# A state-space layer's scan on one core: its convolution summed in PSUM, its decays multiplied into C, and its slots in a new order

## The chip, the cores and the metric

The kernel runs on one core of a Trainium2 chip. The metric is the device time of one execution in microseconds (us). A core has five engines, each with its own queue of instructions that it works off in order: PE (TensorE, matrix products; its weight loads are listed as PEld), DVE (VectorE), ACT (ScalarE), POOL (GpSimd) and SP (SyncE, which here issues DMA transfers). They work on two memories, SBUF and PSUM. PE writes to PSUM, and PSUM has 8 banks of 512 fp32 columns by 128 partitions. An engine waits for another by semaphores.

## The reference

Four layers follow each other on x of shape (4, 128, 64, 64). Only the second is touched. It takes a map of 128 channels through a 1x1 layer, a depthwise 3x3 convolution and silu, then runs two state-space scans (mamba2), forward and backward, over the 4096 pixels of each image:

```python
def _mamba2(u, W_in, conv_w, conv_b, dt_bias, A_log, D, norm_w, W_out):
    zxbcdt = u @ W_in
    z = zxbcdt[..., :DI]
    xBC = zxbcdt[..., DI:DI + DI + 2 * DS]
    dt = zxbcdt[..., -NH:]
    xBC = jax.nn.silu(_causal_dwconv1d(xBC, conv_w, conv_b))
    xs = xBC[..., :DI]
    Bm = xBC[..., DI:DI + DS]
    Cm = xBC[..., DI + DS:]
    dt = jax.nn.softplus(dt + dt_bias)
    dA = jnp.exp(dt * -jnp.exp(A_log))
    xh = xs.reshape(b, l, NH, HD)
    dtx = dt[..., None] * xh
    def step(h, inp):
        dA_t, dtx_t, B_t, C_t = inp
        h = dA_t[:, :, None, None] * h + dtx_t[..., None] * B_t[:, None, None, :]
        y = jnp.einsum('bhpn,bn->bhp', h, C_t)
        return (h, y)
    ...
    y = jnp.moveaxis(ys, 0, 1) + D[None, None, :, None] * xh
    y = y.reshape(b, l, DI)
    y = y * jax.nn.silu(z)
    y = y * lax.rsqrt(jnp.mean(y * y, -1, keepdims=True) + 1e-05) * norm_w
    return y @ W_out

o = jnp.einsum('bihw,io->bohw', x, lin1_w) + lin1_b[None, :, None, None]
o = lax.conv_general_dilated(o, dw_w, (1, 1), 'SAME', ...) + dw_b[None, :, None, None]
o = jax.nn.silu(o)
s = jnp.einsum('bcl,cd->bld', o.reshape(b, c, h * w), fc_in_w)
y1 = _mamba2(s, mam_in_w[0], ...)
y2 = jnp.flip(_mamba2(jnp.flip(s, 1), mam_in_w[1], ...), 1)
```

Here DI = DS = 64 and there is one head. The 4-tap convolution along the sequence is folded into the input projection: S4 holds the features s four times, each shifted by one pixel.

## The kernel before

The second layer is `layer1` (line 1007). Its unit is a group: 512 pixels (4 tiles of 128) of one image, 8 groups an image, 32 in all; the forward direction takes a group's tiles from the front of the image and the backward one from its end, at the same time. One loop (line 1485) works on several groups at once: in iteration G it scans group G, prepares group G+1 (silu of its projections, masks), works out the step lengths of G+2, projects G+3, and convolves the 8-row block G+12 of the maps (`now`), with the blocks next to it as `last` and `nxt`. Each iteration has four slots, j = 0 to 3, one for each tile. `InOrder` (line 74) keeps every engine's instructions in the order in which the program names them, so the order of the calls in a slot is the order of each queue.

The steps, in the words of the prediction:

- `lines` (1111): the 1x1 product (pslin) and its copy to lp by ACT. `conv` (1135): step 0 on ACT, steps 1 to 8 on DVE as scalar_tensor_tensor, each reading lp and the running sum co and writing co, all in SBUF. `conv_silu` (1156) on ACT. `features` (1164): the product pss, then four ACT copies of 32 partitions into S4; with `moved`, used ahead of the loop, one ACT copy and four DMAs on SP (line 1177) in their place.
- `project` (1196) and `take` (1209): the projection pstm of a tile into a bank of the pool mm, and DVE's copies tm and u out of it. `project_c` (1218), `silu_c` (1230): C of a whole group, two products of 512 columns.
- `lengths`, `sums`, `decays`: small work on the step lengths; `decays` gives wd, et and ecs, the exponential of the running sum of the decays. `spans`, `masks`: POOL's products ta, PE's psseg, ACT's exponential lm. `inputs`, `turn_b`, `skips`: xw on POOL, xdt on DVE, the transposes psb of B and DVE's copy B, ACT's product with D.
- The scan of a tile: `pairs` (1347) C times B into CY; `update` (1361) the new part of the state (xw) and C times the old state (hst), then DVE's new state; `weigh` (1355) DVE's lmc; `within` (1380) its product with xdt; `gated` (1387) DVE's y in three instructions (two that multiply C times state by ecs and add tm, one that adds the product of `within`) and POOL's product Y.
- `behind` (1402): the norm and the last product of finished groups, as generators that are taken forward by one step at the end of a slot; all open ones are.

PSUM: the pool mm has 4 buffers of a bank, the two tiles CY (one for even slots, one for odd) have two banks each.

```python
CY = [pp.tile([P, 2, 512], F32, name=f"CY{k}") for k in range(2)]
...
co, lp[:, k // 3:k // 3 + 8, k % 3:k % 3 + HW], dw[:, k:k + 1], co, ALU.mult, ALU.add)
```

Of the kernel before, what the change touches and what calls it, by code (L numbers as in the profile page):

```python
# [17 lines left out]
P = 128  # L18
NB = 4
HW = 64  # L20
# [74 lines left out]
class Kernel:  # L95
# [911 lines left out]
    def layer1(self, after):  # L1007
# [13 lines left out]
        with ExitStack() as ctx:  # L1021
# [5 lines left out]
            pm = ctx.enter_context(tc.tile_pool(name="l1pm", bufs=4, space=PSUM))  # L1027
# [17 lines left out]
            def weights():  # L1045
                ps = mm("psw2")
                nc.tensor.matmul(ps[:, 0:P], out_wT, fc_out, start=True, stop=True)
                nc.vector.tensor_scalar(w2, ps[:, 0:P], self.col("norm_w"), None, ALU.mult)
                taps = gp.tile([P, 2, 192], F32, name="taps", tag="C", bufs=3)
                nc.sync.dma_start(taps, self.ins["taps4"])  # L1050
                nc.vector.tensor_mul(wx[:, :, 0:192], wx[:, :, 0:192], taps)
# [6 lines left out]
            nA = cp.tile([P, 2], F32, name="nA")  # L1058

            def constants():  # L1060
# [11 lines left out]
                nc.vector.tensor_copy(ident_r, self.ident)  # L1072
                nc.scalar.activation(nA, self.row("A_log"), AF.Exp)
# [4 lines left out]
            Y = cp.tile([P, NT + 2 * GS, 2, DI], F32, name="Y")  # L1078

# [55 lines left out]
            def conv(n, b, k):  # L1135
                lp = lps[n, b]
                if k == 0:
                    own = space(n, b)
                    co = own[1] if own else gp.tile([P, 8, HW], F32, name="co")
                    cos[n, b] = co  # L1140
                    nc.scalar.activation(co, lp[:, 0:8, 0:HW], AF.Copy, scale=dw[:, 0:1])
                    return
# [13 lines left out]
            def conv_silu(n, b):  # L1156
                src = cos[n, b]
                if len(src.shape) == 2:
                    src = src.rearrange("p (r c) -> p r c", c=HW)
                    own = space(n, b)  # L1160
                    cos[n, b] = own[1] if own else gp.tile([P, 8, HW], F32, name="co")
                nc.scalar.activation(cos[n, b], src, AF.Silu, bias=self.col("dw_b"))

            def features(n, b, moved=False):
# [9 lines left out]
                for m in range(4):  # L1174
                    ms = slice(32 * m, 32 * m + 32)
                    if moved:
                        plain.sync.dma_start(s[ms, b * 512 + m:b * 512 + m + 512],
                                             cos[n, b][ms].rearrange("p r c -> p (r c)"))
                    else:
                        nc.scalar.copy(s[ms, b * 512 + m:b * 512 + m + 512], ps[ms, :])  # L1180
# [15 lines left out]
            def project(g, j):  # L1196
# [5 lines left out]
                q = groups[g]  # L1202
                ps = mm("pstm")
                psv = ps.rearrange("p (d e) -> p d e", d=2)
                for dr in range(2):
                    nc.tensor.matmul(psv[:, dr, 0:193], s4(g, dr, j), wx[:, dr, 64:257], start=True, stop=True)
                q.pt = psv

            def take(g, j):
                q = groups[g]  # L1210
                psv = q.pt
# [6 lines left out]
            def project_c(g):  # L1218
# [3 lines left out]
                nc.tensor.matmul(q.pc[0:64, :], wx[:, 0, 0:64], s4(g, 0, 0, 512), start=True, stop=True)  # L1222
                nc.tensor.matmul(q.pc[64:128, :], wx[:, 1, 0:64], s4(g, 1, GS - 1, 512), start=True, stop=True)
# [6 lines left out]
            def silu_c(g):  # L1230
                q = groups[g]
                q.C = gp.tile([P, 512], F32, name="C", bufs=3)
                nc.scalar.activation(q.C, q.pc, AF.Silu, bias=self.col("cb_C"))

            def turn_b(g):
# [5 lines left out]
                nc.vector.tensor_copy(q.B, ps)  # L1241
# [3 lines left out]
            def small(name):  # L1245
                return sp.tile(sh, F32, name=name, bufs=4)

            def lengths(g):
# [3 lines left out]
                u, e, w, lg = q.u, small("e"), small("w"), small("lg")  # L1252
# [16 lines left out]
                q.parts = small("lead"), small("rest")  # L1269
# [14 lines left out]
            def sums(g):  # L1284
# [8 lines left out]
                q.cs = small("cs")  # L1293
                q.tot, q.wd = small("tot"), small("wd")
# [5 lines left out]
            def decays(g):  # L1300
                q = groups[g]
                q.ecs = small("ecs")
                q.et = sp.tile([P, GS], F32, name="et", bufs=4)
                nc.scalar.activation(q.ecs, q.cs, AF.Exp)
# [38 lines left out]
            def block(q, dr, j):  # L1343
                b = j if dr == 0 else GS - 1 - j
                return q.C[64 * dr:64 * dr + 64, b * P:(b + 1) * P]

            def pairs(g, j):
                q = groups[g]
                for dr in range(2):
                    nc.tensor.matmul(CY[j % 2][:, dr, 0:P], q.B[64 * dr:64 * dr + 64, j * P:(j + 1) * P],  # L1350
                                     block(q, dr, j), start=True, stop=True)
# [8 lines left out]

            def update(g, j):
# [5 lines left out]
                cy = CY[j % 2]  # L1367
                for dr in range(2):
                    nc.tensor.matmul(cy[64 * dr:64 * dr + 64, 0, 256:320],
                                     q.tm[:, j, 128 + 64 * dr:192 + 64 * dr], q.xw[:, j, dr, :],  # L1370
                                     start=True, stop=True)
                for dr in range(2):
                    nc.tensor.matmul(cy[:, dr, 128:192], block(q, dr, j), state[0][64 * dr:64 * dr + 64, :],
                                     start=True, stop=True)
                h2 = kp.tile([P, DI], F32, name="hst", bufs=3)
                nc.vector.scalar_tensor_tensor(h2, state[0], q.et[:, j:j + 1], cy[:, 0, 256:320],
# [3 lines left out]
            def within(g, j):  # L1380
                q = groups[g]
                lm = weighted.pop((g, j))
                for dr in range(2):
                    nc.tensor.matmul(CY[j % 2][:, dr, 192:256], lm[:, dr, :], q.xdt[:, j, dr, :],
                                     start=True, stop=True)

            def gated(g, j):
                q = groups[g]
                n, i = divmod(g, NG)
                r, cy = GS * i + j, CY[j % 2]  # L1390
                y = kp.tile([P, 2, DI], F32, name="y")
                for dr in range(2):
                    nc.vector.scalar_tensor_tensor(y[:, dr, :], cy[:, dr, 128:192], q.ecs[:, j, dr:dr + 1],
                                                   q.tm[:, j, 64 * dr:64 * dr + 64], ALU.mult, ALU.add)
                nc.vector.tensor_tensor(y, y, cy[:, :, 192:256], ALU.add)
# [87 lines left out]
            for x in left[0:2]:  # L1483
                features(*x, True)
            for G in range(NG + 1 - AHEAD, N + 1):
# [9 lines left out]
                if G >= 1 and i >= NG // 2:  # L1495
                    backs.append(behind(n, NG - 1 - i))
                if later:
                    dts = lengths(G + 2)

                for j in range(GS):  # L1500
                    if now is not None and j == 0:
                        conv(*now, 0)
                    if later and j == 0:
                        project_c(G + 2)
# [3 lines left out]
                    if later and j == 0:  # L1508
                        silu_c(G + 2)
                    if last is not None and j == 0:  # L1510
                        conv_silu(*last)
                    if j == 0 and (later or soon or here):
                        nc.scalar.preload_act_table_set("natural_log_exp_and_others")
                    if here:
                        if j == 0 and G == 0:
                            pairs(0, 0)
                        update(G, j)
                        weigh(G, j)
                    if 0 <= G - 1 < N and j == 0:
                        gated(G - 1, GS - 1)  # L1520
                    if here and j:
                        gated(G, j - 1)
                    if first:
                        project(G + 3, j)
                    if soon and j == 1:
                        masks(G + 1, 0)
                        spans(G + 1, 1)
                        inputs(G + 1)
                        turn_b(G + 1)
                    if soon and j == 2:  # L1530
                        masks(G + 1, 1)
                        skips(G + 1)
                    if later and j in (1, 2):
                        next(dts)
                    if later and j == 3:
                        sums(G + 2)
                    if here:
# [5 lines left out]
                    if now is not None:  # L1543
                        for k in ((1, 2), (3, 4), (5, 6), (7, 8))[j]:
                            conv(*now, k)
                    if first:
                        take(G + 3, j)
                    if nxt is not None and j == 1:
                        lines(*nxt)
                    if last is not None and j == 2:  # L1550
                        features(*last)
                    if later and j == 3:
                        decays(G + 2)
                    for b in list(backs):
# [1346 lines left out]
```

## Time and profile before

| | |
|---|---|
| median of 3 runs | 4906.62 us (4895.81 to 4910.19) |
| the profiled execution, its time | 4906.88 us |
| the profiled execution, its span | 4904.8 us |
| PE busy | 4487.7 us, 91% |
| DVE busy | 3588.3 us, 73% |
| ACT busy | 3608.9 us, 74% |
| POOL busy | 3064.4 us, 62% |
| the second layer in the span | about 816 to 1600 us |
| mean granted PE clock | 0.947 of full speed |

The span is from the first to the last instruction. Busy shares over the whole span mix four layers; only the stretch from 816 to 1600 us says something of this change. In the answers shown below, a group of instructions has its engine, operation, output and inputs by the program's names, shape and count, then its busy time in us and the mean duration of one in ns, then the idle time just before them and what ended it. In a list of stretches the granted clock of PE is the number after the five engines' busy times, and the last two are the DMA share and GB/s. L85 is the line of the helper that issues everything in order.

### The profile page before, as it was taken

What the parts mean: (1) busy time and instruction counts of PE and PEld (TensorE: products, weight loads), DVE (VectorE), ACT (ScalarE), POOL (GpSimd) and SP (SyncE); (2) the same over time, 40 slices, a digit from 0 to 9 for tenths busy, and PEclk for the clock granted to TensorE, in tenths of its full rate; (3) what the DMA queues carried; (4) which work ended last, traced back from release to release, by engine and by line L of the source; (5) the groups of instructions that cost most, each with busy time, mean ns of one, the idle gap of its engine ahead of it and who ended that gap; (6) DMA issues with size and microseconds to landing.
All of it is one profiled execution on the core that took longest, in us unless ns stands there. A gap on an engine that the chain in (4) does not pass through costs nothing. (4 is left out here: it accounts for less than half of the span.)

```text
span 4904.8 us, 65981 instructions
## 1 busy us (share of the span) xinstructions
PE 4487.7 (91%) x22552; PEld 2439.1 (50%) x22552; DVE 3588.3 (73%) x7198; ACT 3608.9 (74%) x5496; POOL 3064.4 (62%) x3043
## 2 busy tenths in 40 slices
PE   6889977888999699997997999999999999999798
PEld 4777765566666344443443444444444444444344
DVE  5999996788876788874775666666666666665675
ACT  4466644555554677775766999999999999999575
POOL 0334443355555345552797888888888888877488
PEclk9999998788788899998999999999999999999899
DMA  6667772000000300000000000000000000000000
GB/s 211 182 187 187 199 185 67 12 9 10 18 12 16 96 5 1 1 1 0 18 35 18 1 1 1 1 1 1 1 1 1 1 1 1 1 1 1 8 28 35
DMA packets 67474, 190.47 MB, mean 39 GB/s; under 512 B 12532, under 2 KB 15796, under 8 KB 65460
## 3 DMA queue, kind: packets, MB, share of 16 engines
q1 hardware_dynamic: 61700, 170.19, 12.2%
q0 software_dynamic: 2240, 12.85, 0.9%
q8 instruction: 182, 2.98, 0.3%
q10 hardware_dynamic: 3184, 3.08, 0.2%
q14 instruction: 168, 1.38, 0.1%
HBM read 133.23 MB, written 50.74 MB: 38 GB/s over the span
## 5 line engine op out<-in xcount | busy, mean ns | idle before, releaser
L85 POOL TENSOR_TENSOR r<-r 128x512 f32<-128x512 f32 (+1 forms) x1088 | 1349.1, 1241 | 331.6 <-DVE r L85 271.4
L85 DVE TENSOR_TENSOR r<-r,num 128x1024 f32<-128x1024 f32 (+1 forms) x1088 | 974.8, 927 | 597.5 <-PE num L85 502.6
L85 PE MATMUL D<-F,G 32*128 32x512 f32 (+3 forms) x4608 | 1139.9, 573 | 1.8 <-DVE den L85 0.9
L85 PE MATMUL num<-F,G 32*128 32x512 f32 (+3 forms) x4608 | 1057.1, 590 | 6.8 <-DVE r L85 3.9
L85 ACT ACTIVATE r<-r 128x2048 f32<-128x2048 f32 (+4 forms) x610 | 1018.6, 1679 | 51.4 <-POOL r L85 4.3
L85 ACT ACTIVATE r<-D 128x1536 f32<-128x1536 f32 (+1 forms) x544 | 763.4, 1403 | 49.6 <-PE D L85 29.3
L85 PEld LDWEIGHTS D<-F,G 32*128 32x128 f32 x4608 | 484.8, 184 | 372.8 <-issue 235.2
L85 PE MATMUL acc<-r,v 128*128 128x512 f32 (+3 forms) x1152 | 598.1, 606 | 0.7 <-ACT r L85 0.7
L85 POOL TENSOR_TENSOR x<-x 128x512 f32<-128x512 f32 (+2 forms) x320 | 405.4, 1267 | 148.5 <-DVE m L85 66.3
L85 PEld LDWEIGHTS num<-F,G 32*128 32x128 f32 x4608 | 383.4, 183 | 223.4 <-issue 111.4
L85 PE MATMUL pff<-hid,w_ffn_w2T 128*128 128x512 f32 x1024 | 468.0, 600 | 0.0
L85 PE MATMUL pex<-w_expert_w,vT 128*128 128x512 f32 x1024 | 462.6, 600 | 1.6 <-DVE x L85 1.4
L85 POOL TENSOR_TENSOR piece<-v,wt 128x512 f32<-128x512 f32 x160 | 167.5, 1064 | 373.3 <-DVE cum L85 91.7
L85 PEld LDWEIGHTS acc<-r,v 128*128 128x128 f32 x1152 | 174.1, 188 | 382.7 <-issue 188.9
L85 PE MATMUL acc<-ident,pr 128*128 128x128 f32 x2560 | 322.0, 284 | 42.0 <-DVE pr L85 42.0
L85 ACT ACTIVATE x<-pex,gate 128x128 f32<-128x128 f32 x896 | 256.6, 367 | 104.0 <-PE pex L85 78.8
L85 PEld LDWEIGHTS acc<-ident,pr 128*128 128x128 f32 x2560 | 299.2, 147 | 55.8 <-DVE pr L85 54.1
L85 ACT ACTIVATE hid<-phh,cols 128x512 f32<-128x512 f32 x416 | 252.8, 688 | 67.1 <-PE phh L85 67.0
L85 PEld LDWEIGHTS pex<-w_expert_w,vT 128*128 128x128 f32 x1024 | 191.2, 193 | 217.2 <-issue 160.7
L85 PEld LDWEIGHTS pff<-hid,w_ffn_w2T 128*128 128x128 f32 x1024 | 184.9, 190 | 200.6 <-issue 200.6
L85 DVE TENSOR_TENSOR pr<-v,near_w 128x2560 f32<-128x2560 f32 x96 | 270.0, 2813 | 5.6 <-PE acc L85 4.8
L85 POOL TENSOR_TENSOR Y<-y,tm 128x64 f32<-128x64 f32 x256 | 111.7, 456 | 236.3 <-DVE y L85 149.2
(495 smaller groups left out, 7916.4 us busy)
## 6 DMA issues: line engine op xcount, KB each, us to landing
v<-tab SPq DMA_DIRECT2D x320, 256.0 KB
oms<-omw SPq DMA_DIRECT2D x32, 432.0 KB
omr<-oms SPq DMA_DIRECT2D x32, 432.0 KB
X<-in_x_dram SPq DMA_DIRECT2D x8, 1024.0 KB
tab<-vb SPq DMA_DIRECT2D x64, 128.0 KB
o<-o SPq DMA_DIRECT2D x32, 256.0 KB
oin<-o SPq DMA_DIRECT2D x32, 256.0 KB
kept<-X SPq DMA_DIRECT2D x4, 2048.0 KB
```

Of the source, the lines that this page charges most:

```text
L85: self.last = op(*args, **kwargs)
```

## The change

Only `layer1` differs. It

- puts the running sum of the convolution, when it is not one of the first blocks, into a PSUM bank of its own (cop), and takes that bank from the pool mm, which has 3 buffers then; `conv_silu` writes its result to co in SBUF, now with one buffer;
- projects a tile into columns 256 to 448 of the CY banks of its slot, in place of a bank of mm;
- makes exp of the running decays for a whole group by products of a matrix of ones with ta (`decay`), multiplies it into C on POOL (Ce), and takes Ce for C times the old state, so that `within` adds its product onto that one in PSUM, and `gated` needs one instruction on DVE; ecs goes;
- stores C in the order of the tiles (eight products of 128 columns), one group later than before, except ahead of an image's last group;
- copies B by ACT; moves the features into S4 by four DMAs inside the loop and by ACT and DVE copies in the last two calls ahead of it (the reverse of before);
- gives small tiles fewer buffers, splits `update` into `state_part`, `update` and `advance`, orders the calls in the slots anew, and takes one open generator of `behind` at a time until the last four groups.

```diff
-            pm = ctx.enter_context(tc.tile_pool(name="l1pm", bufs=4, space=PSUM))
+            pm = ctx.enter_context(tc.tile_pool(name="l1pm", bufs=3, space=PSUM))
...
-                    co = own[1] if own else gp.tile([P, 8, HW], F32, name="co")
+                    co = own[1] if own else pp.tile([P, 512], F32, name="cop").rearrange(
+                        "p (r c) -> p r c", c=HW)
...
+                else:
+                    cos[n, b] = gp.tile([P, 8, HW], F32, name="co", bufs=1)
                 nc.scalar.activation(cos[n, b], src, AF.Silu, bias=self.col("dw_b"))
 
-            def features(n, b, moved=False):
+            def features(n, b, moved=True):
...
+                    elif m < 2:
+                        nc.scalar.copy(s[ms, b * 512 + m:b * 512 + m + 512], ps[ms, :])
                     else:
-                        nc.scalar.copy(s[ms, b * 512 + m:b * 512 + m + 512], ps[ms, :])
+                        nc.vector.tensor_copy(s[ms, b * 512 + m:b * 512 + m + 512], ps[ms, :])
...
-                    nc.tensor.matmul(psv[:, dr, 0:193], s4(g, dr, j), wx[:, dr, 64:257], start=True, stop=True)
-                q.pt = psv
+                    nc.tensor.matmul(CY[j % 2][:, dr, 256:449], s4(g, dr, j), wx[:, dr, 64:257], start=True, stop=True,
+                                     skip_group_check=True)
...
-                nc.tensor.matmul(q.pc[0:64, :], wx[:, 0, 0:64], s4(g, 0, 0, 512), start=True, stop=True)
-                nc.tensor.matmul(q.pc[64:128, :], wx[:, 1, 0:64], s4(g, 1, GS - 1, 512), start=True, stop=True)
+                for j in range(GS):
+                    for dr in range(2):
+                        nc.tensor.matmul(q.pc[64 * dr:64 * dr + 64, j * P:(j + 1) * P], wx[:, dr, 0:64],
+                                         s4(g, dr, j), start=True, stop=True, skip_group_check=True)
...
-                nc.vector.tensor_copy(q.B, ps)
+                nc.scalar.copy(q.B, ps)
...
-                nc.scalar.activation(q.ecs, q.cs, AF.Exp)
...
+            def decay(g, dr):
+
+                q = groups[g]
+                if dr == 0:
+                    q.Ce = gp.tile([P, 512], F32, name="Ce")
+                ps = mm("psrow")
+                for k, ta in enumerate(q.ta):
+                    nc.tensor.matmul(ps, ones_r, ta.rearrange("p j t -> p (j t)"), start=(k == 0), stop=(k == 1))
+                hs = slice(64 * dr, 64 * dr + 64)
+                nc.scalar.activation(q.Ce[hs, :], ps[hs, :], AF.Exp)
+                if dr == 1:
+                    nc.gpsimd.tensor_tensor(q.Ce, q.Ce, q.C, ALU.mult)
...
+            def state_part(g, j):
+                q = groups[g]
+                for dr in range(2):
+                    nc.tensor.matmul(CY[j % 2][64 * dr:64 * dr + 64, 0, 192:256],
+                                     q.tm[:, j, 128 + 64 * dr:192 + 64 * dr], q.xw[:, j, dr, :],
+                                     start=True, stop=True, skip_group_check=True)
...
-                    nc.tensor.matmul(cy[:, dr, 128:192], block(q, dr, j), state[0][64 * dr:64 * dr + 64, :],
-                                     start=True, stop=True)
+                    nc.tensor.matmul(CY[j % 2][:, dr, 128:192], block(q.Ce, dr, j), state[0][64 * dr:64 * dr + 64, :],
+                                     start=True, stop=False, skip_group_check=True)
+
+            def advance(g, j):
...
-                    nc.tensor.matmul(CY[j % 2][:, dr, 192:256], lm[:, dr, :], q.xdt[:, j, dr, :],
-                                     start=True, stop=True)
+                    nc.tensor.matmul(CY[j % 2][:, dr, 128:192], lm[:, dr, :], q.xdt[:, j, dr, :],
+                                     start=False, stop=True, skip_group_check=True)
...
-                for dr in range(2):
-                    nc.vector.scalar_tensor_tensor(y[:, dr, :], cy[:, dr, 128:192], q.ecs[:, j, dr:dr + 1],
-                                                   q.tm[:, j, 64 * dr:64 * dr + 64], ALU.mult, ALU.add)
-                nc.vector.tensor_tensor(y, y, cy[:, :, 192:256], ALU.add)
+                nc.vector.tensor_tensor(y, q.tm[:, j, 0:128].rearrange("p (d e) -> p d e", d=2),
+                                        CY[j % 2][:, :, 128:192], ALU.add)
...
             for x in left[0:2]:
-                features(*x, True)
+                features(*x, False)
```

The slots after the change, with the calls in order (a number behind a call is its slot where it is not in all four):

```python
one_by_one = G < N - NG // 2
...
conv_silu(last) 0; conv(now, 0) 0; spans(G + 1, 0) 0; silus(G + 1) 0
state_part(G, j); project(G + 3, j); update(G, j)
project_c(G + 1) 0; silu_c(G + 1) 0; preload of the exponential's table 0
gated(the tile before)
conv(now, 4) 1, (now, 6) 2, (now, 7) 3
advance(G, j); weigh(G, j); take(G + 3, j)
masks(G + 1, 0) 1; decay(G + 1, 0) 1; spans(G + 1, 1) 1; inputs 1; turn_b 1; masks(G + 1, 1) 2; decay(G + 1, 1) 2
lengths(G + 2) 1 and 2; conv(now, 8) 3; sums(G + 2) 3; skips(G + 1) 3; lines(nxt) 2
features(last) 3, or 2 for an image's last block
within(G, j); pairs(the next tile)
conv(now, 1, 2, 3) 0, (now, 5) 1
decays(G + 2) 3; one step of behind
```

## The prediction

> **What bounds the kernel now.** I read the page's busy parts first, then the second layer by stage, its groups of instructions by form between 1000 and 1400 us, and the order of time. The profiled run took 4906.88 us, 2.1 us more than its span of 4904.8 us and 0.3 us from the median of 4906.62 us (4895.81 to 4910.19), so the sum below is added straight to the median. The changed layer is a serial stretch, from its loads (816) to its statistics (about 1600 us); what it gains or loses, the kernel does.
>
> Busy time by stage (us of stretch, then PE, PEld, DVE, ACT, POOL, then the granted clock):
>
> ```profile
> 816.00:885.00 69.00, 51.33 (x111) 24.03 (x112) 43.62 (x69) 25.49 (x40) 10.37 (x49) 0.83 0.17 41
> 885.00:916.10 31.10, 23.14 (x93) 13.85 (x91) 25.81 (x71) 24.73 (x45) 10.82 (x15) 0.83 0.00 1
> 916.10:1386.20 470.10, 417.58 (x2179) 288.38 (x2179) 404.33 (x1092) 263.82 (x491) 244.81 (x374) 0.79 0.03 10
> 1386.20:1588.20 202.00, 185.43 (x1176) 135.72 (x1176) 140.25 (x508) 101.78 (x197) 113.40 (x183) 0.86 0.04 15
> ```
>
> The rows are the convolutions ahead of the loop, its three iterations without a scan, the 20 groups that scan and also convolve (23.5 us each), and the 12 that scan alone (16.8). In the third row PE (89%) and DVE (86%) are both nearly full, PE at a clock of 0.79. Why the clock is low, four stretches inside one group show:
>
> ```profile
> 1239.90:1246.70 6.80, 6.80 (x43) 4.95 (x42) 6.51 (x13) 3.79 (x8) 6.72 (x9) 1.00 0.01 2
> 1246.70:1250.10 3.40, 0.51 (x3) 0.07 (x1) 3.40 (x9) 1.63 (x4) 0.69 (x4) 1.00 0.06 22
> 1250.10:1260.40 10.30, 10.21 (x36) 6.98 (x36) 7.43 (x29) 4.26 (x12) 3.33 (x6) 0.50 0.12 44
> ```
>
> For 3.4 us PE stands still while DVE is full; then the clock is 0.50 for 10.3 us and PE is the slow engine. DVE causes the stop, the half clock prolongs it. What DVE did there, in order of time:
>
> ```profile
> 1243.36 0.96 DVE L85 TENSOR_SCALAR w<-e 128x8 f32<-128x8 f32 x1
> 1244.24 3.06 DVE L85 SCALAR_TENSOR_TENSOR co<-lp,cols,co 128x512 f32<-128x512 f32 x2
> ...
> 1250.19 1.12 PE L85 MATMUL CY<-xdt,lmc 128*128 128x64 f32 x4 [2.98 <-DVE lmc L85]
> ```
>
> Two convolution steps took 3.06 us, since POOL works on SBUF beside them; alone such a step takes 0.752 us, the median of the 192. Between 1000 and 1400 us (17 groups):
>
> ```profile
> L85 DVE SCALAR_TENSOR_TENSOR co<-lp,cols,co 128x512 f32<-128x512 f32 x130 | 132.9, 1022 | 2.3
> L85 ACT COPY S<-pss 32x512 f32<-32x512 f32 x68 | 39.2, 577 | 57.1 <-PE pss L85 56.5
> L85 DVE SCALAR_TENSOR_TENSOR y<-CY,ecs,tm 128x64 f32<-128x64 f32 x137 | 32.0, 274 | 0.0
> L85 PE MATMUL psseg<-ta,later_r 128*128 128x512 f32 x68 | 28.4, 494 | 0.6 <-POOL ta L85 0.5
> L85 PE MATMUL psc<-S,w_in_w 128*64 128x512 f32 x68 | 27.4, 899 | 0.0
> L85 DVE COPY B<-psb 128x512 f32<-128x512 f32 x17 | 11.6, 682 | 4.6 <-PE psb L85 4.6
> ```
>
> **DVE's part, per group.** The sum in PSUM: 8 steps fall from 1022 to 752 ns if POOL then leaves them alone, 2.2 us. No row shows DVE write to PSUM. Reading it is free: xdt from SBUF alone (128x512, median 685 ns) and lmc and y with a PSUM input (128x256 in 412, 128x128 in 287) all lie 146 to 154 ns above 1.04 ns a column, the slope up to the first layer's 128x2560 product with near_w (2813). ACT writes 128x480 into PSUM (near_w) in 560 ns, no dearer than its 128x512 copies at 577 to 586. Bounds for a step: 741 ns, the fastest row, and 752 + 512 x 1.04 = 1285 ns if reading and writing one bank take turns; I take 752, which both reads and ACT's write point to. Taking ecs into C removes 8 y steps of 274 ns (one addition of 287 per tile remains): 2.2 us, about 1.9 back to back. The copy of B goes to ACT: 0.7. So DVE falls from 20.2 to some 15.5 us per group.
>
> [...]
>
> **PE's part, per group.** The decay rows for Ce are two products per direction of the kind psseg<-ta: 4 x 28.4/68 = 1.7 us. project_c goes from 4 passes of 512 columns (27.4/17 = 1.6 us) to 16 of 128; at the scan's 128-column row (CY<-C,B, 41.2 us for 272) these are 2.4, at the same streaming rate 1.6; I take +0.6. Together +2.3 at clock 0.79, or +1.8 at full clock (bounds 1.3 and 2.0). PE's work is now 417.58 x 0.79/20 = 16.5 us at full clock, then 18.3.
>
> **ACT and POOL.** ACT loses 4 copies of 0.577 and ecs (0.2), gains one 128x512 copy, B (0.586 each) and two exponentials of 0.6: about +0.1 on 13.2 of 23.5. POOL gains one product of 1.04 on 12.2. Both are covered by the 23.5 us period, and still at 19; uncovered, POOL's 1.04 would delay update through Ce.
>
> **Queues and waits.** features now sends its copy by four DMAs on SP, 0.588 us each to issue. The last pair ahead of the loop shows the length of this: the ACT copy ends at 874.1, eight issues run to 878.0, PE starts at 879.59. For four I count 1.9 to the last issue and 2.1 from it, 4.0 us. As co has one buffer, conv_silu at the head of the next iteration waits for them, and it stands first on ACT: conv step 0, silus, silu_c, the table load and the masks' exponentials queue behind it, and DVE's conv steps 1 to 3 wait for step 0. Ring at full clock: conv step 1 to take(3) on DVE some 12.5 us, product and copy 0.9 later, DMA 4.0, silu 0.71, step 0 0.72: 19 us. It is below PE's figure but leaves a hole of some 2 to 3 us in DVE. Moreover within must now wait for take, which reads the bank it writes (pairs already waits for y on another part of CY: 0.2 us, 24 times), and mm has three buffers, so psb waits for silu_c.
>
> **The sum.** PE work at full clock divided by the period is 16.5/23.5 = 0.70 in these groups; in the densest stretch of the scan alone (1400 to 1550: 139.70 busy of 150 at 0.93) it is 0.87. With DVE at 15.5 the group moves toward the second, but the ring, within's wait and the backs keep it short: I take 0.85, so 18.3/0.85 = 21.5, a gain of 2.0 x 20 = 40 us (0.87: 49; 0.78: none). The 12 scan-only groups are PE's already for nine (1386 to 1536.6: 142.17 of 150.40): +1.8 each, 16, less 4 that backs taken one at a time fill into PE's gaps: +12 (bounds 0 and 25); the last three (51.6 us at 0.67) wait in turn and stay. The iterations ahead: the 5.80 us wait of PE at 879.59 goes (copies instead of DMAs, 4 x 0.577 on two engines: net -4), while three rings lose some 3 us each: +5 (bounds -4 and 9). Net -40 + 12 + 5 = -23: **4884 us**, own range 4862 to 4898.
>
> **Rivals.** (1) DVE was the whole trouble, chance 0.20: PE's 3 us stops go, the clock stays near 1, and the ring's 19 us and some 1 us of backs set the group: 20.0, gain 70, less 12 and 5: 4854. For it: nearly all half-clock stretches begin behind a stop on lmc. Against: the ring leaves another stop. (2) PE becomes the bound at the low clock, chance 0.22, and this is the slower side: conv step 1 waits for the DMA, lmc(1) is late by 3 us, PE stops there once per group as now, and the clock halves as at 1250. Then utilisation stays near 0.75: 18.3/0.75 = 24.4, +18, with +12 and +5: 4942. It decides from 0.78 down for a group, and from 0.81 down for the total (18.3/0.81 = 22.6, a gain of 18, which the +17 around it eat). (3) Accumulating in PSUM costs 1285 ns, chance 0.10: DVE gains 1.9 + 0.7 - 2.1 and stays near 19.7, the group near 23.3: -4 + 17, 4920. (4) The parts cancel, chance 0.06: 4906.
>
> **How the numbers follow.** The forecast holds 0.42. Under 0.3% (14.7 us, about what a measurement of this kernel tells from no change) lies some of its range: it gives 0.29 faster and 0.13 same. With 0.20 faster; 0.20 slower and 0.02 same; 0.08 and 0.02; 0.03 same and 0.03 slower: faster 0.49, same 0.20, slower 0.31. The range reaches to rivals 1 and 2 with the unknown costs: 4838 to 4938.
>
> **What would show it.** co's steps on DVE at 752 ns with hardly any above 900 (the sum in PSUM right); a mean near 1285 makes rival 3. The clock over the 20 groups above 0.79, and PE's waits on lmc shorter than 50 us in 400; ACT waiting for S's DMA ahead of conv_silu by 1 to 3 us per group; four new products of 0.3 to 0.4 us per group. I am wrong if the 20 groups stay above 23 us, or fall below 20, or if the scan-only groups gain.

## The result, and the profile after

The changed kernel takes 4979.88 us (median; 4979.27 to 4981.50), the kernel before, measured with it, 4901.36 (4895.81 to 4910.19): 78.5 us more, ratio 1.0159, 95% interval 1.0140 to 1.0178. It is slower, above the range and on the side of rival 2. The profiled execution has a span of 4978.3 us against 4904.8.

Busy time by stage in the kernel after (us of stretch, then PE, PEld, DVE, ACT, POOL, then the granted clock): the 20 groups that scan and convolve, the nine that scan and project, the last three.

```profile
925.30:1412.40 487.10, 421.53 (x2500) 298.29 (x2500) 321.96 (x914) 255.77 (x469) 224.10 (x396) 0.86 0.07 20
1412.40:1599.80 187.40, 172.71 (x1094) 129.86 (x1094) 103.59 (x342) 97.68 (x180) 96.94 (x151) 0.84 0.04 15
1599.80:1658.90 59.10, 49.67 (x266) 35.24 (x264) 21.87 (x61) 23.49 (x41) 28.31 (x44) 0.65 0.04 14
```

Before, the stretches were 470.1, 150.4 and 51.3 us, and the loop began at 916.1. So 17.0 us were lost in the 20 groups (24.4 us each in place of 23.5), 37.0 in the nine, 7.8 in the three and 9.2 ahead. DVE's work in the 20 groups did fall, from 404.33 to 321.96 us, and the clock rose from 0.79 to 0.86. The nine groups, which have no convolution, went the other way: clock 0.93 to 0.84.

Groups of instructions between 1000 and 1400 us (busy us, mean ns of one, idle time just before them and what ended it):

```profile
L85 DVE SCALAR_TENSOR_TENSOR cop<-lp,cols,cop 128x512 f32<-128x512 f32 x132 | 99.0, 750 | 36.3 <-ACT cop L85 35.1
L85 PE MATMUL CY<-xdt,lmc 128*128 128x64 f32 x260 | 44.4, 299 | 34.6 <-DVE u L85 34.5
L85 ACT ACT_TABLE_LOAD x33 | 42.3, 1283 | 35.0 <-DMA S<-co 34.7
L85 PE MATMUL psrow<-ta,ones_r 128*128 128x512 f32 x66 | 25.8, 479 | 3.5 <-ACT C L85 3.5
L85 PE MATMUL psc<-S,w_in_w 128*64 128x128 f32 x256 | 20.5, 310 | 0.0
L85 DVE TENSOR_TENSOR y<-tm,CY 128x128 f32<-128x128 f32 x65 | 18.0, 277 | 11.1 <-PE CY L85 7.7 <-POOL lp L85 1.4 <-POOL Ce L85 1.4
```

Each instruction costs what the prediction said: a step of the sum 750 ns, one y of 277 ns a tile, the decay's products 0.39 us each. What is new stands in the last column. The waits of the same 400 us (us in total, times, longest):

```profile
PEld CY L85 <- DVE u L85: 50.3, 44, 3.9
DVE hst L85 <- PE CY L85: 44.3, 35, 3.0
DVE cop L85 <- ACT cop L85: 35.1, 14, 3.3
ACT L85 <- DMA S<-co: 34.7, 14, 3.6
PE CY L85 <- DVE u L85: 34.5, 31, 3.7
DVE tm L85 <- POOL Y L85: 13.1, 10, 3.4
```

Before, PE and PEld waited in the same place, ahead of `within`, 41.5 and 50.6 us for lmc. That wait is gone, and one for u, the end of `take`, stands there, nearly as long. In order of time, one group's turn shows it (start, us, engine, instruction, idle time before it):

```profile
946.29 0.58 ACT L85 COPY co<-pss 128x512 f32<-128x512 f32 x1 [2.54 <-PE pss L85]
...
946.90 2.41 SPq L1188 DMA_DIRECT2D S<-co  x4
...
949.85 0.56 DVE L85 TENSOR_TENSOR tm<-CY,rows 128x384 f32<-128x384 f32 x1 [0.65 <-POOL Y L85]
...
950.53 0.66 PE L85 MATMUL CY<-xdt,lmc 128*128 128x64 f32 x4 [0.96 <-DVE u L85]
950.84 1.28 ACT L85 ACT_TABLE_LOAD   x1 [3.56 <-DMA S<-co]
...
952.14 0.69 ACT L85 ACTIVATE co<-cop,cols 128x512 f32<-128x512 f32 x1
...
952.92 0.69 ACT L85 ACTIVATE cop<-lp,cols 128x512 f32<-128x512 f32 x1
...
953.64 2.34 DVE L85 SCALAR_TENSOR_TENSOR cop<-lp,cols,cop 128x512 f32<-128x512 f32 x3 [3.17 <-ACT cop L85]
...
955.64 0.66 PE L85 MATMUL psb<-ident,tm 128*128 128x128 f32 x4 [1.19 <-ACT C L85]
...
956.75 0.27 DVE L85 SCALAR_TENSOR_TENSOR hst<-hst,et,CY 128x64 f32<-128x64 f32 x1
...
957.94 0.67 PE L85 MATMUL CY<-xdt,lmc 128*128 128x64 f32 x4 [1.65 <-DVE u L85]
```

ACT's copy into co ends at 946.87; ACT goes on at 950.84, when the four DMAs have read it, and then first with 1.28 us of table load for the silu. DVE idles 3.17 us, runs its three steps, and only behind them (and behind y and a fourth step) come the state's step, the weighing and `take`, so the next `within` starts at 957.94. Three groups later, the same turn in four stretches (columns as by stage):

```profile
1023.30:1026.70 3.40, 2.71 (x17) 1.79 (x14) 1.38 (x2) 3.29 (x5) 0.00 (x0) 1.00 0.00 0
1026.70:1030.10 3.40, 1.17 (x8) 0.94 (x8) 3.36 (x9) 3.37 (x6) 2.21 (x4) 1.00 0.00 0
1030.10:1037.00 6.90, 6.90 (x25) 4.93 (x25) 4.94 (x20) 1.70 (x5) 2.76 (x5) 0.51 0.01 2
1037.00:1043.80 6.80, 6.31 (x45) 4.62 (x44) 3.32 (x11) 3.12 (x8) 2.76 (x8) 1.00 0.17 41
```

PE is busy 1.17 of 3.40 us, and for the next 6.9 us the clock is 0.51: the mechanism of before, with another cause.

### The profile page after: what moved, and what is told of

Same layout as the page of the kernel before. It is cut to its first block, busy times and chain, and to the rows that moved or that the text cites. A ratio compares the mean times of both kernels' runs of the same rounds, so it can differ in the third digit from the quotient of the medians.

```text
span 4978.3 us, 67067 instructions
## 1 busy us (share of the span) xinstructions
PE 4527.7 (91%) x23064; PEld 2474.9 (50%) x23064; DVE 3490.6 (70%) x6915; ACT 3614.1 (73%) x5490; POOL 3054.0 (61%) x3075
## 5 line engine op out<-in xcount | busy, mean ns | idle before, releaser
L85 POOL TENSOR_TENSOR Y<-y,tm 128x64 f32<-128x64 f32 x256 | 76.6, 320 | 183.3 <-DVE y L85 183.1
```

What stands on the lines that cost most here:

```text
L85: self.last = op(*args, **kwargs)
```

## The experiments

Theories at the start. A: the new waits, the ring through co's DMAs and `take` ahead of `within`, cost the time. B: PE's added work does. C: taking the backward parts one at a time does. Later ones are named where they come up. All runs follow. The runs were spread over several chips, so "less before" takes off the median of the kernel before that was measured with each (4901.36 us for the changed kernel, 4892 to 4897 for the others), and differences between runs are differences of that column. The ratio and its interval are those on record; the ratio need not be the quotient of the two medians. The stretches and the clock are from one profiled execution each, whose time lies up to 11 us from its run's median; that of the kernel before took 4906.88 us.

| run | median us | less before | ratio, 95% interval | 20 groups | nine | clock in the 20 |
|---|---|---|---|---|---|---|
| before | | 0 | 1 | 470 | 150 | 0.79 |
| after | 4979.88 | +78.5 | 1.0159 [1.0140, 1.0178] | 487 | 187 | 0.86 |
| e1 copies | 4968.78 | +74.0 | 1.0156 [1.0139, 1.0173] | 472 | 191 | 0.84 |
| e2 take late | 4965.88 | +71.1 | 1.0150 [1.0133, 1.0167] | 484 | 171 | 0.84 |
| e3 no decay products | 4974.39 | +79.6 | 1.0166 [1.0149, 1.0183] | 491 | 186 | 0.80 |
| e4 all backs | 4972.36 | +77.5 | 1.0162 [1.0145, 1.0179] | 476 | 189 | 0.88 |
| e5 e1 and e2 | 4931.35 | +38.8 | 1.0084 [1.0069, 1.0098] | 449 | 175 | 0.89 |
| e6 e5, projection behind | 5096.63 | +204.1 | 1.0417 [1.0403, 1.0432] | 602 | 181 | 0.75 |
| e7 sum alone | 4845.30 | -47.3 | 0.9910 [0.9896, 0.9924] | 402 | 149 | 0.90 |
| e8 sum and decays | 4883.28 | -9.3 | 0.9985 [0.9975, 0.9994] | 421 | 162 | 0.91 |
| e9 e8, shared banks | 5042.59 | +148.1 | 1.0308 [1.0290, 1.0327] | 530 | 214 | 0.77 |
| e10 e8, features by DMA | 4890.15 | -4.3 | 0.9987 [0.9979, 0.9996] | 433 | 169 | 0.87 |
| e11 after, own bank | 4989.51 | +95.1 | 1.0183 [1.0164, 1.0201] | 504 | 174 | 0.81 |
| e12 e7, B on ACT | 4856.75 | -37.7 | 0.9913 [0.9899, 0.9928] | 422 | 146 | 0.85 |
| e13 e5, own bank | 4945.15 | +51.1 | 1.0103 [1.0087, 1.0118] | 469 | 173 | 0.85 |
| e14 e13, weigh first | 4939.98 | +45.9 | 1.0092 [1.0077, 1.0108] | 451 | 185 | 0.90 |
| e15 e5, weigh first | 4927.00 | +32.9 | 1.0073 [1.0059, 1.0087] | 434 | 189 | 0.92 |
| e16 e7, backs apart | 4871.20 | -22.9 | 0.9956 [0.9942, 0.9969] | 423 | 156 | 0.84 |
| e17 e5, B on DVE, backs together | 4917.78 | +20.4 | 1.0043 [1.0029, 1.0057] | 440 | 180 | 0.90 |
| e18 e17, C at the head | 4908.52 | +11.8 | 1.0018 [1.0005, 1.0031] | 432 | 175 | 0.94 |

**One part of the change undone (e1 to e4).** The features of the loop by copies; `take` behind `within`, the pairs and the slot's steps; the decay's products and exponentials away; all backward parts in each slot:

```diff
-            def features(n, b, moved=True):
+            def features(n, b, moved=False):
...
-                    elif m < 2:
+                    elif m < (2 if (n, b) in ((0, 6), (0, 7)) else 4):
```

> The loop's features go into S4 by four ACT copies again, no DMAs; all else as changed. Theory A (waits): the two waits, conv_silu on the DMAs out of co and within on take, make the loss. Then the wait of 3.6 us on the DMA in each of the 20 convolving groups goes, conv step 1 comes about 3 us earlier, those groups fall from 24.4 to about 22 us: near 4935, the scan-only groups unchanged. Theory B (PE work): the added products are the loss; then ACT's 1.7 us more per group bring nothing: 4975 to 4985. Theory C (one generator of behind at a time stretches the end): 4975 to 4985.

```diff
-                    if first:
-                        take(G + 3, j)
...
                         conv(*now, k)
+                    if first:
+                        take(G + 3, j)
```

> take is called behind within, pairs and the convolution's steps of its slot, as before the change, and the projection stays in CY's banks; so within no longer waits for take. Theory A: PE's waits on DVE u (43 us in the convolving groups, 11 in the others) go, the clock of the scan-only groups rises from 0.79 toward 0.86 and they fall from 20.5 to about 18 us each: near 4940. Theory B: at most 10 us less, 4970. Theory C: at most 10 us less.

```diff
-                ps = mm("psrow")
...
-                nc.scalar.activation(q.Ce[hs, :], ps[hs, :], AF.Exp)
...
-                    nc.gpsimd.tensor_tensor(q.Ce, q.Ce, q.C, ALU.mult)
+                    nc.gpsimd.tensor_tensor(q.Ce, q.C, q.C, ALU.mult)
```

> The four products with ones_r per group and the two exponentials into Ce are left out, and POOL multiplies C by C (so the decays are missing from the output); order and waits stay. Theory A: their own 1.3 us at full clock in nine scan-only groups and a part of it elsewhere: 4955 to 4965. Theory B: most of the loss goes, below 4930. Theory C: 4955 to 4970.

```diff
-                    for b in backs[0:1] if one_by_one else list(backs):
+                    for b in list(backs):
```

> All open generators of behind go forward in every slot, as before the change. Theory C: the scan-only groups lose the stretching, 246 to about 225 us: near 4958. Theories A and B: within 10 us of 4980, either way.

None of the four gives the loss back: each ratio's interval overlaps that of the changed kernel (e4 came out as A and B had it, the other three outside all their cases). In the stretches, e1 took 15 us off the 20 groups, e4 11, and e2 16 off the nine. In e3 PE had less to do, and the clock in the 20 groups fell from 0.86 to 0.80: the work removed was given back. So none of A, B, C is the loss by a single part.

**Two waits at once, and the projection moved (e5, e6).** e5 is e1 with e2; e6 also puts the projection behind the weighing, where it was, but leaves it in the pairs' banks:

```diff
-                    if first:
-                        project(G + 3, j)
                     if here:
                         update(G, j)
...
                         weigh(G, j)
+                    if first:
+                        project(G + 3, j)
```

> The changed kernel with both edits of the first two experiments: features by four copies, and take behind within and the conv steps. Theory A (the waits, but one hides behind the other, so that each edit alone shows little): the conv groups fall well below the 472 us of the copies alone, to about 455, the nine scan-only groups to about 171; 4935 or less. Theory D (the loss is in the new slot order and work, not in these waits): the two add as they came alone, 11 + 14 us: about 4955, conv groups 468.

> As e5, and the projection's products go back to their place behind the weighing (still into the pairs' banks), so that update and the state's step no longer stand behind them. Theory A (waits in the shared bank): the nine scan-only groups fall from 171 to the 150 of the kernel before, conv groups by another 10: about 4910. Theory D: within 8 us of e5.

e5 took back 40 us where its parts took 5 and 7: in the 20 groups 38, against 15 and 3. The two waits lie beside each other, and either alone keeps the groups long. PE's longest waits from 930 to 1330 us show it, for e1 (one line), e2 (three) and e5 (one):

```profile
PE CY L85 <- DVE u L85: 39.9, 23, 4.8
...
PE CY L85 <- DVE lmc L85: 18.7, 15, 2.4
PE psb L85 <- ACT C L85: 16.1, 8, 2.3
PE psrow L85 <- ACT C L85: 7.9, 6, 2.1
...
PE CY L85 <- DVE lmc L85: 23.1, 18, 2.6
```

Without the DMAs PE still waits for `take`; with `take` late it waits for ACT's C, which stands behind the wait on the DMAs in ACT's queue (24.0 us, and 2.6 in e5). That is A, and D falls. e6 was a miss by 187 us and shows what the shared bank does. One row of e6 between 1000 and 1400:

```profile
L85 PE MATMUL CY<-w_in_w,S 128*128 128x193 f32 x216 | 67.5, 449 | 103.5 <-DVE lmc L85 103.5
```

The projection now comes behind DVE's read for lmc in the same bank. It writes columns 256 to 448 and lmc reads 0 to 127, and yet PE stands 103.5 us of 400 for it. Ahead of `update`, as in the changed kernel, this wait does not occur, but the state's step has the projection in front of it in PE's queue.

**From the other end: parts of the change alone (e7, e8).** e7 is the kernel before with the sum in one PSUM bank, three buffers in mm, and conv_silu ahead of step 0:

```diff
-            pm = ctx.enter_context(tc.tile_pool(name="l1pm", bufs=4, space=PSUM))
+            pm = ctx.enter_context(tc.tile_pool(name="l1pm", bufs=3, space=PSUM))
...
-                    co = own[1] if own else gp.tile([P, 8, HW], F32, name="co")
+                    co = own[1] if own else pp.tile([P, 512], F32, name="cop").rearrange(
+                        "p (r c) -> p r c", c=HW)
```

> The kernel before with one part of the change: the convolution's sum in one PSUM bank (three banks left for the short products, and conv_silu ahead of the next block's step 0, as one bank demands). Nothing else moves. The prediction's reading (a conv step falls from 1022 to 752 ns and VectorE's share of the period sets the time): gain of about 2.2 us in each of 20 groups less what three banks cost, 4855 to 4875. Rival S (with one bank step 0 waits for conv_silu, and the period is set by the chain, not by VectorE's work): 4890 or more, though the steps take 752 ns.

e8 adds Ce, the two products that add in PSUM, the single y, C by tiles for G+1, and the smaller buffers, all in the old slots:

```diff
                         masks(G + 1, 0)
+                        decay(G + 1, 0)
...
-                    if later and j == 0:
-                        project_c(G + 2)
+                    if soon and j == 0 and (G + 1) % NG < NG - 1:
+                        project_c(G + 1)
...
-                    nc.tensor.matmul(CY[j % 2][:, dr, 192:256], lm[:, dr, :], q.xdt[:, j, dr, :],
-                                     start=True, stop=True)
+                    nc.tensor.matmul(CY[j % 2][:, dr, 128:192], lm[:, dr, :], q.xdt[:, j, dr, :],
+                                     start=False, stop=True, skip_group_check=True)
```

> As e7, and C times its tile's decays with two products adding in PSUM, C projected tile by tile one group later, in the order of slots of the kernel before: everything of the change but the projections in the pairs' banks, the features by DMA, B's copy on ScalarE and the new slots. If the loss comes from those four (theory A or the new order): 4850 to 4885, and the scan-only groups stay near the 150 + 52 of the kernel before. If the decays and C's sixteen passes are what costs (theory B): 4920 or more, with the scan-only groups up by 20 or more.

e7 is 10 us better than the prediction's reading gave, and rival S falls. e8 lies inside its first case, though its nine groups grew. Stages of e7, then of e8:

```profile
923.40:1325.80 402.40, 366.44 (x2179) 256.13 (x2180) 350.99 (x1092) 262.76 (x489) 198.00 (x374) 0.90 0.03 11
1325.80:1474.30 148.50, 140.21 (x950) 104.24 (x950) 113.15 (x422) 83.81 (x164) 86.96 (x143) 0.95 0.04 15
```

```profile
924.70:1345.60 420.90, 384.83 (x2499) 283.97 (x2499) 333.41 (x933) 283.84 (x509) 223.89 (x394) 0.91 0.03 11
1345.60:1507.70 162.10, 153.59 (x1094) 121.46 (x1094) 102.81 (x351) 94.06 (x174) 99.70 (x151) 0.91 0.04 14
```

The sum alone gains 47 us (4892.57 to 4845.30), and PE's waits for lmc fall away: 6.1 us in 400, 41.9 before. DVE's step of 752 ns, none slower than 0.76 us, goes with it; the other two edits of e7, which one bank asks for, were not run apart from it. The decays, with C by tiles and the smaller buffers, then cost 38, nearly work for work: PE's busy time at the granted clock goes from 366.44 x 0.90 / 20 = 16.5 to 384.83 x 0.91 / 20 = 17.5 us a group, and the nine groups grow by 13.6.

**What e8 lacks, one part at a time (e9 to e12).** e9 puts the projections into the pairs' banks (ahead of update, `take` behind y); e10 lets the loop's features go by DMA; e11 gives the changed kernel's projection a bank of mm again; e12 adds B's copy on ACT to e7:

```diff
-                    nc.tensor.matmul(psv[:, dr, 0:193], s4(g, dr, j), wx[:, dr, 64:257], start=True, stop=True)
+                    nc.tensor.matmul(CY[j % 2][:, dr, 256:449], s4(g, dr, j), wx[:, dr, 64:257], start=True, stop=True,
+                                     skip_group_check=True)
```

> e8 and one more part of the change: the projections go into the pairs' banks, with the products ahead of update and take behind the y of the slot before, so that PE and DVE must take turns in a bank within each slot. Theory E (the shared bank is the largest of the parts that lie between e8's 4883 and the changed kernel's 4980): +40 to +80, 4925 to 4965, scan-only groups up by 20 or more, within waiting for u. Theory F (the DMA ring and the new order carry the loss): 4875 to 4900.

```diff
-            def features(n, b, moved=False):
+            def features(n, b, moved=True):
```

> e8 and one more part of the change: the features of the loop go by one copy into co's only buffer and four DMAs. Theory F: conv_silu waits for the DMAs that read co, step 0 and the table load stand behind it: +1.5 to +2.5 us in each of 20 groups, 4910 to 4935. Theory E, or a ring hidden where the features are issued at the third slot and not the fourth: ScalarE saves three copies a group, 4870 to 4890.

```diff
+                q.pt = mm("pstm").rearrange("p (d e) -> p d e", d=2)
...
-                    nc.tensor.matmul(CY[j % 2][:, dr, 256:449], s4(g, dr, j), wx[:, dr, 64:257], start=True, stop=True,
-                                     skip_group_check=True)
+                    nc.tensor.matmul(q.pt[:, dr, 0:193], s4(g, dr, j), wx[:, dr, 64:257], start=True, stop=True)
```

> The changed kernel with one part undone: the projection's products go to a short bank of their own (three of these for everything), all orders as in the changed kernel. Theory E: 40 to 80 us come back, 4900 to 4940, nine scan-only groups from 187 to 155-165. Theory F: 4965 or more, since the ring stands, and three short banks are one more wait.

```diff
-                nc.vector.tensor_copy(q.B, ps)
+                nc.scalar.copy(q.B, ps)
```

> e7 (the sum alone) with one more part: B's copy out of PSUM on ScalarE, 0.7 us off VectorE in each of 32 groups. VectorE was busy 16.9 of the 17.4 us of e7's shortest groups, ScalarE 11.8. If VectorE's work sets these groups: a gain of 5 to 15, 4830 to 4840. If the copy behind ScalarE's exps holds turn_b's bank or the pairs: 4845 to 4860.

Theories E and F share out the 88 us between e8 and the changed kernel: E to the shared bank, F to the ring and the new order. e9 cost 157 us, twice the upper end of E. Its waits from 930 to 1330 us:

```profile
DVE hst L85 <- PE CY L85: 116.0, 41, 4.8
PEld CY L85 <- DVE u L85: 67.6, 44, 3.1
PE CY L85 <- DVE u L85: 57.0, 34, 3.0
```

Within a slot PE writes a bank, DVE reads it, PE writes it again, and each waits for the other. e10 costs nothing (its ratio is that of e8): the features are issued in the third slot there, and ACT's list of waits has no DMA in it; in the changed kernel they are issued in the fourth, just ahead of the conv_silu that waits for them. e11 came out as F had it: with a bank of its own but the new order nothing comes back. It doesn't price the shared bank by itself, though. `within` no longer waits for u, but the projection now takes one of mm's three buffers, and PE waits for one of these until ACT has read C out of its own (930 to 1330 us):

```profile
PE psrow L85 <- ACT C L85: 23.4, 9, 3.8
...
PE psseg L85 <- ACT C L85: 6.6, 4, 2.1
```

So PE's 34.7 us for u went, but its waits for C grew from 12.8 to 30.0, and the bank and the order can't be priced apart as single terms. e12 lies in the second of its cases: DVE's work was less, the time no better, and the ratios don't separate it from e7.

**The bank crossed with the order (e13 to e16).** e13 is e5 with the bank of e11. e14 and e15 put the state's step and the weighing ahead of y and of the convolution's step, with and without that bank:

```diff
+                    if here:
+                        advance(G, j)
+                        weigh(G, j)
                     if 0 <= G - 1 < N and j == 0:
                         gated(G - 1, GS - 1)
                     if here and j:
                         gated(G, j - 1)
                     for k in steps[:1] if j else ():
                         conv(*now, k)
-                    if here:
-                        advance(G, j)
-                        weigh(G, j)
```

> e5 (the changed kernel with features by copies and take late) with the projection in a short bank of its own: against e8 only the new order of slots and B's copy on ScalarE are left. Theory E (the shared bank is the rest of the loss): 4880 to 4900. Theory G (the order is: y and a convolution step ahead of the state's step and the weighing, so that lmc and with it PE's second product come later in each slot): 4920 to 4940, as e5.

> e13 with the state's step and the weighing ahead of y and the convolution step again, as in the kernel before. Theory G: 15 to 40 us below e13, near e8's 4883. Theory E: within 8 us of e13.

> e5 with the state's step and the weighing first, projections still in the pairs' banks. Theory E: 4930 to 4950, no better than e5, as the state's step then waits longer for the projection in its bank. Theory G: 15 to 40 us below e5.

In the new order a bank of its own, taken from mm's three, gains nothing (e13 against e5, e14 against e15: 12 and 13 us slower by the medians), and the state's step and the weighing put first gain 5 to 6 us; the intervals separate none of these. So neither E, as far as such a bank can test it, nor G (the order) is the rest of the loss. e16 is e7 with the backward parts one at a time:

```diff
-                    for b in list(backs):
+                    for b in backs[0:1] if G < N - NG // 2 else list(backs):
```

> e7 with one more part of the change: the backward parts one at a time up to group 23. In e7 the groups with two of them at work take 22 to 23 us against 17.4 to 18 in the quiet ones, and the part does not lessen the work but spreads it. If work sets these groups: 4840 to 4850. If the bursts stop PE and halve its clock: 4825 to 4835.

It cost 24 us, though no work was added, and lies outside both cases. Its 20 groups, beside e7's 402.40 us at 0.90:

```profile
918.30:1341.40 423.10, 388.24 (x2179) 270.88 (x2180) 359.01 (x1092) 262.11 (x488) 198.06 (x374) 0.84 0.03 10
```

PE's work at the granted clock is the same (388.24 x 0.84 against 366.44 x 0.90, 326 and 330 us), the clock is lower. Some of it is not the edit's: up to group 4 no backward part is at work and the calls of e7 and e16 are the same, yet these five groups took 95.0 us in e7's profile and 100.9 in e16's. One of them took 17.4 us at a clock of 1.00 in e7 and 20.3 at 0.75 in e16. Why the clock differs there, and why the spread lowers it further, stays open.

**The rest (e17, e18).** e17 is e5 with B's copy on DVE and all backward parts together; e18 also puts project_c and silu_c at the head of slot 0, as in e8:

```diff
+                    if soon and j == 0:
+                        if (G + 1) % NG < NG - 1:
+                            project_c(G + 1)
...
                         silus(G + 1)
+                        silu_c(G + 1)
```

> e5 (the changed kernel, features by copies, take late) with two more parts undone: B's copy on VectorE, and all backward parts that wait in each slot. If these two cost here what they cost on top of e7 (11 and 26 us): 4890 to 4900. If the spread of the steps and the later products carry the rest: 4915 or more.

> e17 with C's sixteen passes and its silu at the head of slot 0, as in e8, instead of behind update. If the late C holds a short bank and the products that come after it (psrow and psb waited 5 to 7 times for C's silu in the changed kernel): 4890 to 4905, and the nine scan-only groups fall from 180 towards the 162 of e8. If the spread of steps and the later products carry the rest: 4912 to 4925.

e17 gives 18 us, which the intervals separate from e5, and lies in the second of its cases: on the changed order these two parts cost less than on e7 (10 and 24). e18 gives 9, not separated from e17, between its two cases.

**The account.** From the changed kernel's 78.5 us down: the two waits together 40 us, B and the backward parts 18, C's place some 9, and 21 (from e18's +11.8 to e8's -9.3) that no run here prices: the spread of the convolution's steps, the later products and copies, the projection ahead of update. From e8 down: the decays, with what came with them, 38. What is left, the sum in PSUM, is the gain, and e7 is the fastest kernel of the study: 0.9910 [0.9896, 0.9924] of the kernel before. A second buffer for co, and the features in the third slot of the changed kernel, were not tried.

## Why the prediction was wrong

**DVE's part** was right. 750 ns a step against 752; 16.1 us a group against 15.5. (The lower bound of 741 ns, called the fastest row, is 739 in the trace; nothing rests on it.) The 132 steps with the sum in PSUM took 750 ns each in the mean, and the median one of the 192 in SBUF alone, before, 752: this shape shows no difference between the two.

**PE's and ACT's parts** were right: PE 421.53 x 0.86 / 20 = 18.1 us a group at full clock against 18.3, ACT 255.77/20 = 12.8 against 13.3 (the terms listed for ACT add up to -0.1 and not to the +0.1 that was written). C's sixteen passes took 20.5/16 = 1.3 us a group, not dearer than the four before (1.6), where 0.6 had been added.

**Queues and waits** were seen, and sized nearly right one by one: 4.0 us through the DMAs (measured 3.97), a hole of 2 to 3 us in DVE (3.17). The table load of 1.28 us behind that wait was missed. The iterations ahead of the loop lost 9.2 us, at the upper bound of 9; e7 and e8, which keep their old features there, lose 7 to 9 as well (the loop begins at 923.4 and 924.7), so the rings need not be the cause. One profile does not settle a term of this size: e7 and e16, the same up to there, begin 5.1 us apart.

**The step that failed** is the next one, "the ring, within's wait and the backs keep it short: I take 0.85". It turned two waits, a changed order and a lower work of DVE into one guessed ratio. The measured ratio of PE's work to the period is 18.1/24.4 = 0.74. 0.85 is near what the kernel has without them: e8, in the old order, has 384.83 x 0.91 / 420.9 = 0.83, 21.0 us a group where 21.5 was forecast, and 12.6 us lost in the 12 scan-only groups where 12 were. That its median is 4883 where 4884 was forecast is luck: it is 9 us below the kernel before measured with it, where 23 were forecast, and it lacks part of the change. The sum priced the changed instructions fairly and the new order at almost nothing: the 20 groups lost 17 us where 40 were to be gained, a miss of 57.

**The scan-only term** failed in the same way: +12 forecast, 44.8 measured (37.0 and 7.8), a miss of 33. PE's work in the nine grew as forecast, by 13 us at full clock (142.17 x 0.93 to 172.71 x 0.84, against 16), so what was missed is waiting and the lower clock. `take` ahead of `within` was named as a wait and given no price there; e2 gets 16 us of the nine groups back by moving it. "Less 4 that backs taken one at a time fill into PE's gaps" was not there: undone in the changed kernel (e4) it leaves the nine groups at 189 us against 187, and put alone on e7 (e16) it costs 24 us, 8 of them in the nine.

**Rival 2** named the mechanism: conv step 1 waits for the DMA, PE stops once a group, the clock halves, 0.75, 24.4 us a group. That is what the trace shows in the 20 groups (above: PE busy 1.17 of 3.40 us, then a clock of 0.51). That it is right to the number is partly luck, as its DMA is one of two causes: e1 without the DMA is no better by its interval, since `take` holds the groups as long. Its total of 4942 was 38 us short, as it took the scan-only term over, and it lay above the stated range, which was said to reach it. Rival 1 (DVE the whole trouble, groups of 20.0 us) comes near e7 (20.1 us, though at a clock of 0.90), not the change. Rival 3 fell with the 750 ns.

**The signs that were named** misled in part: the clock rose above 0.79 and the waits on lmc went, both as for the forecast, while the groups grew. The wait had only changed its name, from lmc to u. The sign of being wrong spoke rightly: the 20 groups stayed above 23 us, at 24.4.

## What to carry to other kernels

Price a new order of work as its own part of a change, by walking one period of it with every queue, and not by a ratio of busy time to period; where two new waits lie side by side, undo both before judging either. In this kernel a product waited for a read of its PSUM bank though the columns differ (e6, 103.5 us of 400), so walk the writes and reads of a shared bank too. Moving `take` behind `within` gave 35 us back (e5 against e1); a bank of its own out of three gave none (e11, e13, e14); in e11 PE then waited 30.0 us for ACT's C, 12.8 in the changed kernel. When a change has many parts, run the cheapest one alone: here a few lines of it beat the whole by 126 us, each taken against the kernel before measured with it.

## What the runs showed of the hardware that was not expected

- Less work for PE went with a lower clock: without the decay's products (e3) the 20 groups ran at 0.80 in place of 0.86 and took 491 us in place of 487 in the profiled executions; over the whole kernel its four runs had 0.939 to 0.944, the changed kernel's 0.946 to 0.949.
- POOL gained by DVE's move: in e7 its 374 instructions of the 20 groups took 198.00 us, 244.81 before, with nothing of POOL changed. From 1000 to 1400 us one of its xw took 1039 ns there and 1409 before, one of its Y 370 and 515, and a step on DVE 752 and 1022. What of the move frees both engines, no run shows.
- In the changed kernel conv_silu's wait stands on the table load ahead of it (at 950.84 3.56 us, then 1.28 us of loading), so the load is not hidden by the wait.
